# In-degrees of a graph layer: a stationary tile of ones and moving counts in place of products of two columns and transposes

## The chip, the cores and the metric

The kernel runs on one core of a Trainium2 chip. The metric is device time in microseconds (us), the median of several runs. A core has a tensor engine (PE, or TensorE; its weight loads are listed apart as PEld), a vector engine (DVE, or VectorE), a scalar engine (ACT, or ScalarE), GpSimd (POOL) and a sync engine (SP) that here issues the weight transfers. Each engine works through its own list of instructions in order and waits on semaphores for the others. Matrix products accumulate in PSUM, which has eight banks of 128 partitions x 512 float32 values.

## The reference, cut to what matters

One layer of a graph transformer on 625 nodes of 1024 features with 20000 edges: a layer norm, two graph convolutions beside a linear attention, then a mixture of experts. What the change touches is the in-degree of every node and its inverse:

```python
deg = segment_sum(ones_like(edge_dst), edge_dst, num_segments=N)     # N = 625
deg_inv = 1.0 / maximum(deg, 1.0)
h = relu(sage(x, src, dst, deg_inv, W_self0, W_neigh0, b0))
out = sage(h, src, dst, deg_inv, W_self1, W_neigh1, b1)
# sage: h @ W_self + (segment_sum(h[src], dst) * deg_inv[:, None]) @ W_neigh + b
```

Beside it stands the attention, whose queries and values are computed while the degrees are:

```python
q = softmax(q, axis=-1) * DH ** -0.5
k = softmax(k, axis=-2)
attn = q @ (k.T @ v) ; attn @ Wo + bo
```

## The kernel before, in words

The edges are counted into a matrix `ath` of 625 x 625 counts: `ath[source in tile s, s, destination]`, source nodes in partitions in five tiles (the last has 113 rows), destinations along the free dimension. The sum over an edge's sources is then a product with `ath`, and the in-degree of a destination is the sum of its column.

Every weight matrix passes through a stream: SP loads a block of 512 KB (`wraw`), ScalarE rounds it (`whi`), VectorE forms the rest (`wlo`), each in a ring of three buffers, and TensorE makes three products per pair of tiles (L206 to L208: high with high, low with high, high with low). `ts_half` computes one half (512 columns) of a product for all five node tiles in four units; a unit takes one block of weights and makes thirty products of 512 columns, six for each node tile. Five PSUM banks hold its sums, so three banks are left for everything else at that time. After each unit it can call a `step`.

The order of the stages around the change is: `unpack` (the counts become `ath`), the first half of the queries (`psq`), the second half with `queries_step` after each unit, the first half of the values (`psv`) and the second, with `values_step`; then the context product (`psc`, L727), the query product (`psa`, L744) and later the aggregation (`psag`, L804), which multiplies by `dinv` (L817), and the second convolution, which multiplies by `degs[:, 2]` (L874).

- `queries` (L665) is the softmax of a query half on VectorE and ScalarE: it reads each `psq` bank twice (L671, L672), which sets the bank free, and leaves five tiles `q`.
- `queries_back` (L658) transposes a `q` tile with four TensorE transposes (L662) into `psqt`; ScalarE copies it into `qt`. Each `step` takes two tiles.
- `degrees` (L546), called after unit 0 of the second query half, makes 25 products with a tile of `ath` stationary and two columns of ones moving, so that the degrees of a node tile come out in its own partitions, one column per tile. Two copies and `inverse_degrees` (four steps of `recip` behind a maximum, on 128 x 5) give `degs[:, 2]`.
- `look` (L559), after unit 1, sums the degrees and takes the largest packed count through two transposes and sets the flag `rare`, which is 1 or 2 if the packed counts did not hold the edges. All engines load the flag (L732) and branch on it (L733); the branch is not taken with these inputs.
- `inverse` (L627), after units 2 and 3 of the second half of the values, spreads 1/degree to all partitions with the destinations along the free dimension: five transposes of a broadcast column (L631) and two ScalarE copies give `dinv`.

A planner orders the instructions of each engine from the program's priorities, its dependences and its own estimates of times. PSUM tiles take any bank that is free at their turn.

Of the kernel before, what the change touches and what calls it, by code (L numbers as in the profile page):

```python
# [9 lines left out]
F32 = mybir.dt.float32  # L10
F32R = mybir.dt.float32r
# [5 lines left out]
ALU = mybir.AluOpType  # L17
AX = mybir.AxisListType

N = 625  # L20
T = 128
NT = -(-N // T)
NP = N + 1
# [25 lines left out]
PARTS = ((0, 314), (314, 312))  # L49
# [4 lines left out]
def rows(t):  # L54

    return slice(0, min(T, N - t * T))


def cols(t):

    return slice(t * T, min((t + 1) * T, N))
# [10 lines left out]
def gps_layer(ctx: ExitStack, tc: tile.TileContext, x, src, dst,  # L72
              ws0, wn0, b0, ws1, wn1, b1, wq, wk, wv, wo, bo,
              router_w, w1, w2, sgu, sdown, sgw, out):
    nc = tc.nc

    const = ctx.enter_context(tc.tile_pool(name="const", bufs=1))
    big = ctx.enter_context(tc.tile_pool(name="big", bufs=6))
    wts = ctx.enter_context(tc.tile_pool(name="wts", bufs=3))
    tmp = ctx.enter_context(tc.tile_pool(name="tmp", bufs=5))  # L80
# [12 lines left out]
    def bank(name="ps"):  # L93
        return psum.tile([128, 512], F32, name=name, tag="ps")
# [139 lines left out]
    ident = const.tile([128, 128], F32, name="ident")  # L234
# [56 lines left out]
    def recip(dsttile, a, scratch):  # L291
        nc.vector.reciprocal(dsttile, a)
        nc.vector.scalar_tensor_tensor(scratch, dsttile, -1.0, a, op0=ALU.mult, op1=ALU.mult)
        nc.vector.tensor_scalar(scratch, scratch, 2.0, None, op0=ALU.add)
        nc.vector.tensor_mul(dsttile, dsttile, scratch)
# [128 lines left out]
    with tc.high_priority():  # L424
# [38 lines left out]
                                 op0=ALU.mult, op1=ALU.add))  # L463
# [61 lines left out]
    ath = atp.tile([128, NT, XP], F32R, name="ath")  # L525
    degs = const.tile([128, 5, NT], F32, name="degs")
    nc.gpsimd.memset(degs, 0.0)
    two = const.tile([128, 2], F32R, name="two")
    nc.vector.memset(two.bitcast(F32), 1.0)

    def unpack():
        for s in range(NT - 1, 0, -1):
# [9 lines left out]
    def inverse_degrees():  # L542
        nc.vector.tensor_scalar(degs[:T, 1, :], degs[:T, 0, :], 1.0, None, op0=ALU.max)
        recip(degs[:T, 2, :], degs[:T, 1, :], degs[:T, 3, :])

    def degrees():  # L546
        ps = bank("psdg")
        for t in range(NT):
            for s in range(NT):
                nc.tensor.matmul(ps[rows(t), 2 * t:2 * t + 2], ath[rows(s), s, cols(t)], two[rows(s)],  # L550
                                 start=s == 0, stop=s == NT - 1)
        for a, b in ((0, NT - 1), (NT - 1, NT)):
            nc.vector.tensor_copy(degs[rows(a), 0, a:b],
                                  ps[rows(a), 2 * a:2 * b].rearrange("p (t k) -> p t k", k=2)[:, :, 0])
        inverse_degrees()

    rare = const.tile([1, 1], I32, name="rare")

    def look():  # L559


        nc.vector.reduce_sum(degs[:T, 4, 0:1], degs[:T, 0, :], axis=AX.X)
        ps = bank("psdm").rearrange("p (a b) -> p a b", b=128)
        for k in range(2):
            nc.tensor.transpose(ps[:1, k, :T], degs[:T, 4, k:k + 1], ident[:T, :T])
        few = const.tile([1, 2], F32, name="few")
        nc.vector.reduce_sum(few[:, 0:1], ps[:1, 0, :T], axis=AX.X)
        nc.vector.reduce_max(few[:, 1:2], ps[:1, 1, :T], axis=AX.X)
        nc.vector.tensor_scalar(few[:, 0:1], few[:, 0:1], float(E), None, op0=ALU.is_lt)
        nc.vector.scalar_tensor_tensor(rare, few[:, 1:2], 16.0, few[:, 0:1], op0=ALU.is_ge, op1=ALU.add)  # L570

    ard = dram.tile([NT * WIN, NP], F32, name="ard")
    atd = dram.tile([N, NP], F32R, name="atd")
# [1 line left out]
    def recount():  # L575

        acc = tmp.tile([128, NP], F32, name="acc", tag="tmp")
        sep = tmp.tile([128, 2, HW], F32, name="sep", tag="tmp")
        ct = tmp.tile([128, HW], F32, name="ct", tag="tmp")
        nc.vector.tensor_tensor(edst, edst, first_dst[:ET, None, :, None].to_broadcast([ET, 2, NG, CH // 2]), op=ALU.add)  # L580
        nc.vector.tensor_scalar(field[:ET], esrc, float(HW), None, op0=ALU.is_ge)
        nc.vector.scalar_tensor_tensor(esrc, field[:ET], -float(HW), esrc, op0=ALU.mult, op1=ALU.add)
        nc.vector.tensor_scalar(field[:ET], field[:ET], 4095.0, 1.0, op0=ALU.mult, op1=ALU.add)
        with tc.For_i(0, NT, 1) as r:
            nc.vector.memset(acc, 0.0)
            with tc.For_i(0, NG, 1) as g:
                ps = bank("pa")
                for i in range(CH):
                    h = tmp.tile([128, WIN + HW + 1], F16, name="hrare", tag="tmp")
                    nc.vector.tensor_scalar(h[:ET, :WIN], iota[:ET, :WIN], edst[:, i // 8, ds(g, 1), i % 8], None, op0=ALU.is_equal)  # L590
                    nc.vector.tensor_scalar(h[:ET, WIN:WIN + HW], iota[:ET, :HW], esrc[:, i // 8, ds(g, 1), i % 8],
                                            field[:ET, i // 8, ds(g, 1), i % 8], op0=ALU.is_equal, op1=ALU.mult)
                    nc.tensor.matmul(ps[:, :HW], h[:ET, :WIN], h[:ET, WIN:WIN + HW], start=i == 0, stop=i == CH - 1)
                nc.scalar.activation(ct, ps[:, :HW], AF.Identity, bias=mid, scale=2.0 ** -12)
                nc.vector.tensor_scalar(sep[:, 1, :], ct, MAGIC, None, op0=ALU.subtract)
                nc.vector.scalar_tensor_tensor(sep[:, 0, :], sep[:, 1, :], -4096.0, ps[:, :HW],
                                               op0=ALU.mult, op1=ALU.add)
                nc.vector.tensor_add(acc, acc, sep.rearrange("p a s -> p (a s)"))
            nc.gpsimd.dma_start(ard[ds(r * WIN, WIN), :], acc)
            nc.vector.tensor_scalar(edst, edst, float(WIN), None, op0=ALU.subtract)  # L600
        for j in range(NT):
            aj = tmp.tile([128, NP], F32, name="aj", tag="tmp")
            nc.gpsimd.dma_start(aj[rows(j)], ard[cols(j), :])
            for s in range(NT):
                ps = bank("psat")
                nc.tensor.transpose(ps[rows(s), rows(j)], aj[rows(j), cols(s)], ident[rows(j), rows(j)])
                al = tmp.tile([128, T], F32R, name="al", tag="tmp")
                split(ps[rows(s), rows(j)], ath[rows(s), s, cols(j)], al[rows(s), rows(j)])
                nc.gpsimd.dma_start(atd[cols(s), cols(j)], al[rows(s), rows(j)])
        for t in range(NT):  # L610
            pt = bank("psdt")
            for s in range(NT):
                al = tmp.tile([128, T], F32R, name="al", tag="tmp")
                nc.gpsimd.dma_start(al[rows(s), rows(t)], atd[cols(s), cols(t)])
                nc.tensor.matmul(pt[rows(t), :2], ath[rows(s), s, cols(t)], two[rows(s)], start=s == 0, stop=False)
                nc.tensor.matmul(pt[rows(t), :2], al[rows(s), rows(t)], two[rows(s)], start=False, stop=s == NT - 1)
            nc.vector.tensor_copy(degs[rows(t), 0, t:t + 1], pt[rows(t), 0:1])
        inverse_degrees()

# [7 lines left out]
    def inverse(t0, n):  # L627
        ps = bank("psd").rearrange("p (a b) -> p a b", b=128)
        for t in range(n):
            p = rows(t0 + t)  # L630
            nc.tensor.transpose(ps[:, t, p], degs[p, 2, t0 + t:t0 + t + 1].to_broadcast([p.stop, 128]), ident[p, p])  # L631
        c = slice(t0 * T, min((t0 + n) * T, N))
        nc.scalar.copy(dinv[:, c], ps.rearrange("p a b -> p (a b)")[:, :c.stop - c.start])
# [50 lines left out]
    def queries_step(u):  # L684
        for a in (next(back, None), next(back, None)):
            if a:
                queries_back(*a)
        if u == 0:
            degrees()
        elif u == 1:  # L690
            look()

    accs = [bank("psq") for _ in range(NT)]
    ts_half(xnh, xnl, accs, step=queries_step)
    back = iter(list(queries(1, accs)))
    mid_ctx = ExitStack()
    midp = mid_ctx.enter_context(tc.tile_pool(name="midp", bufs=1))
    dinv = midp.tile([128, NP], F32, name="dinv")


    def values_step(half, u):
        if half == 0:
            for a in (next(back, None), next(back, None)):
                if a:
                    queries_back(*a)
        elif u > 1:
            inverse(*((0, NT - 1), (NT - 1, 1))[u - 2])

    vnat = None
    for half in range(2):  # L710
# [12 lines left out]
    for o in range(KT):  # L723
        ps = bank("psc")
# [15 lines left out]
    for o in range(KT):  # L740
        for c0, n in PARTS:
            n = min(n, N - c0)
            ps = bank("psa")
# [9 lines left out]
    for half in range(2):  # L753
# [3 lines left out]
        for t in range(NT):  # L757
            xr = tmp.tile([128, 512], F32, name="xr", tag="tmp")
            p = rows(t)
# [18 lines left out]
    with tc.If(rare_v > 0, preferred_fallthrough_block=False):  # L778
        for s in range(NT):
            al = low_part(s)  # L780
            for o in range(KT):
                for c0, n in PARTS:
                    ps = bank("pslo")
                    c = slice(c0, min(c0 + n, N))
                    nc.tensor.matmul(ps[:, :n], g0h[rows(s), s, o * 128:(o + 1) * 128], al[rows(s), c0:c0 + n],
                                     start=True, stop=True)
# [42 lines left out]
    for half in range(2):  # L829
# [3 lines left out]
        for t in range(NT):  # L833
            p = rows(t)
# [3 lines left out]
    with tc.If(rare_v > 0, preferred_fallthrough_block=False):  # L838
        for s in range(NT):
            al = low_part(s)  # L840
            for t in range(NT):
                for half in range(2):
                    hs = slice(half * 512, (half + 1) * 512)
                    ps = bank("pslo")
                    p = rows(t)
# [396 lines left out]
    for i, r in enumerate(RANKS):  # L1242
        between = None
        if i < NE - 1:
            n = CAPS[RANKS[i + 1]]
# [73 lines left out]
```

## Time and profile before

| what | value |
|---|---|
| median of 3 runs | 1025.9 us (1025.32 to 1026.54) |
| the profiled execution's own time | 1026.03 us |
| its span, first to last instruction | 1024.5 us |
| mean granted clock of TensorE | 0.996 of full speed |
| TensorE busy | 1003.0 us, 98% |
| VectorE busy | 595.5 us, 58% |
| ScalarE busy | 395.4 us, 39% |
| GpSimd busy | 147.8 us, 14% |

The second query half begins at 177.85 us, the values at 211.9, their second half at 241.52, the context product at 269.29 and the query product at 279.22.

A line of the order of time gives the start, the duration (both in us), the engine, the line of the kernel, the operation and the tiles as out<-in; "128*128 128x2" is the stationary tile and then the output. Matrix products overlap, so that the distance from one start to the next is what one costs, not its duration. In a line of a group, the figures behind the bar are the busy time in us and the mean duration of one in ns, and then the engine's idle time ahead of them and what ended it. In a line of waits the figures are the total in us, how often, and the longest. In a line of stretches each engine has its busy time and number of instructions, in the order PE, PEld, DVE, ACT, POOL; then come the granted clock, the share of the transfer engines that was busy, and GB/s.

### The profile page before, as it was taken

What the parts mean: (1) busy time and instruction counts of PE and PEld (TensorE: products, weight loads), DVE (VectorE), ACT (ScalarE), POOL (GpSimd) and SP (SyncE); (2) the same over time, 40 slices, a digit from 0 to 9 for tenths busy, and PEclk for the clock granted to TensorE, in tenths of its full rate; (3) what the DMA queues carried; (4) which work ended last, traced back from release to release, by engine and by line L of the source; (5) the groups of instructions that cost most, each with busy time, mean ns of one, the idle gap of its engine ahead of it and who ended that gap; (6) DMA issues with size and microseconds to landing.
All of it is one profiled execution on the core that took longest, in us unless ns stands there. A gap on an engine that the chain in (4) does not pass through costs nothing. (4 is left out here: it accounts for less than half of the span.)

```text
span 1024.5 us, 14773 instructions
## 1 busy us (share of the span) xinstructions
PE 1003.0 (98%) x5557; PEld 863.4 (84%) x5557; DVE 595.5 (58%) x1207; ACT 395.4 (39%) x579; POOL 147.8 (14%) x206
## 2 busy tenths in 40 slices
PE   8999999999999999999999999999999989999998
PEld 6889998888878888988878999997978777887786
DVE  7999643572333325533337355458686788887681
ACT  5443242232221122222115332345646566766610
POOL 1000001110045100200001004213030033210120
PEclk9999999999999999999999999999999999999999
DMA  8022227664235321322230137566877898897861
GB/s 230 21 82 64 83 97 250 213 220 131 72 121 168 130 83 63 122 78 67 82 83 2 43 83 267 139 196 191 277 240 230 262 293 285 292 285 248 324 264 51
DMA packets 111464, 164.68 MB, mean 161 GB/s; under 512 B 5931, under 2 KB 63443, under 8 KB 111382
## 3 DMA queue, kind: packets, MB, share of 16 engines
q1 hardware_dynamic: 97734, 118.38, 36.8%
q0 software_dynamic: 13456, 45.08, 13.1%
q8 instruction: 47, 0.77, 0.3%
q14 instruction: 35, 0.29, 0.1%
q10 hardware_dynamic: 192, 0.16, 0.0%
HBM read 133.19 MB, written 30.42 MB: 160 GB/s over the span
## 5 line engine op out<-in xcount | busy, mean ns | idle before, releaser
L97 DVE TENSOR_TENSOR wlo<-wraw,whi 128x1024 fp32r<-128x1024 f32 x149 | 188.3, 1264 | 271.2 <-ACT whi L97 266.5
L97 ACT CAST whi<-wraw 128x1024 fp32r<-128x1024 f32 x149 | 156.6, 1051 | 310.5 <-PE psg L208 66.2
L1157 PE MATMUL pse<-xs,whi 128*128 128x448 f32 (+1 forms) x384 | 109.0, 357 | 0.0
L97 DVE TENSOR_TENSOR wlo<-wmore,whi 128x1024 fp32r<-128x1024 f32 x67 | 86.9, 1298 | 28.7 <-ACT whi L97 27.7
L1153 PE MATMUL pse<-xs,wlo 128*128 128x224 f32 (+1 forms) x384 | 89.7, 254 | 0.8 <-DVE wlo L97 0.8
L97 ACT CAST whi<-wmore 128x1024 fp32r<-128x1024 f32 x67 | 70.4, 1051 | 48.4 <-PE psz L208 17.9
L396 PE MATMUL psk<-xnh,whi 128*128 128x314 f32 (+3 forms) x256 | 82.5, 323 | 0.7 <-ACT xnh L97 0.7
L397 PE MATMUL psk<-xnl,whi 128*128 128x314 f32 (+3 forms) x256 | 79.7, 311 | 0.6 <-DVE xnl L97 0.6
L398 PE MATMUL psk<-xnh,wlo 128*128 128x314 f32 (+3 forms) x256 | 79.4, 310 | 0.0
L1153 PEld LDWEIGHTS pse<-xs,wlo 128*128 128x128 f32 x384 | 72.0, 190 | 1.9 <-DVE wlo L97 1.0
L1209 PE MATMUL psy<-wlo,he 128*128 128x512 f32 (+1 forms) x176 | 70.0, 398 | 3.3 <-DVE wlo L97 2.9
L1157 PEld LDWEIGHTS pse<-xs,whi 128*128 128x128 f32 x384 | 69.0, 189 | 2.4
L1208 PE MATMUL psy<-whi,he 128*128 128x512 f32 (+1 forms) x176 | 69.4, 395 | 0.0
L1210 PE MATMUL psy<-whi,he 128*128 128x512 f32 (+1 forms) x176 | 69.1, 392 | 0.0
L476 DVE TENSOR_SCALAR hot<-iota,srow,unit 125x128 f16<-125x128 f16 x160 | 51.7, 323 | 0.0
L97 POOL TENSOR_TENSOR xs<-raw,xs 128x512 fp32r<-128x512 f32 (+2 forms) x24 | 34.4, 1452 | 118.6 <-ACT xs L97 97.4
L396 PEld LDWEIGHTS psk<-xnh,whi 128*128 128x128 f32 x256 | 49.1, 192 | 1.2 <-ACT xnh L97 1.2
L397 PEld LDWEIGHTS psk<-xnl,whi 128*128 128x128 f32 x256 | 49.3, 193 | 0.8 <-DVE xnl L97 0.8
L398 PEld LDWEIGHTS psk<-xnh,wlo 128*128 128x128 f32 x256 | 49.1, 192 | 0.0
L1209 PEld LDWEIGHTS psy<-wlo,he 128*128 128x128 f32 (+1 forms) x176 | 31.8, 180 | 14.9 <-DVE wlo L97 6.7
L475 DVE TENSOR_SCALAR hot<-iota,edt 125x128 f16<-125x128 f16 x160 | 41.9, 262 | 0.2 <-issue 0.2
L1208 PEld LDWEIGHTS psy<-whi,he 128*128 128x128 f32 (+1 forms) x176 | 31.9, 181 | 10.1
(347 smaller groups left out, 2331.0 us busy)
## 6 DMA issues: line engine op xcount, KB each, us to landing
wraw<-in_L_ffn_w_dram SPq DMA_DIRECT2D x65, 512.0 KB, 5.0
wmore<-in_L_ffn_w_dram SPq DMA_DIRECT2D x63, 512.0 KB, 5.5
xsd<-zt POOLq DMA_DIRECT2D x9, 1024.0 KB
wraw<-in_L_gnn_W_self_dram SPq DMA_DIRECT2D x16, 512.0 KB, 3.9
wraw<-in_L_gnn_W_neigh_dram SPq DMA_DIRECT2D x16, 512.0 KB, 3.8
wraw<-_ffn_shared_gate_up_dram SPq DMA_DIRECT2D x16, 512.0 KB, 3.9
wraw<-in_L_mix_Wk_dram SPq DMA_DIRECT2D x8, 512.0 KB, 6.8
wraw<-in_L_mix_Wq_dram SPq DMA_DIRECT2D x8, 512.0 KB, 3.6
```

Source lines behind the costliest of these rows:

```text
L97: return (order(nc.scalar.copy(hi, srcap)), order((eng or nc.vector).tensor_sub(lo, srcap, hi.bitcast(F32))))
L396: nc.tensor.matmul(ps[:, :n], wh[:, kt, :], xnh[:, kt, c], start=kt == 0, stop=False)
L397: nc.tensor.matmul(ps[:, :n], wh[:, kt, :], xnl[:, kt, c], start=False, stop=False)
L398: nc.tensor.matmul(ps[:, :n], wl[:, kt, :], xnh[:, kt, c], start=False, stop=kt == KT - 1)
L475: nc.vector.tensor_scalar(h[:ET, :WIN], iota[:ET, :WIN], edst[e], None, op0=ALU.is_equal)
L476: return nc.vector.tensor_scalar(h[:ET, WIN:], iota[:ET, :WIN], srow[e], unit[e].bitcast(F32), op0=ALU.is_equal, op1=ALU.mult)
L1153: nc.tensor.matmul(ps[a][:, :n], wl[:, k, c], xs[:, kt, 0, :], start=False, stop=False)
L1157: nc.tensor.matmul(ps[a][:, :2 * n], wh[:, k, c], xs[:, kt], start=kt == 0, stop=kt == KT - 1)
L1208: nc.tensor.matmul(acc, h(kt, 0), wh[:, k, :], start=kt == 0, stop=False)
L1209: nc.tensor.matmul(acc, h(kt, 0), wl[:, k, :], start=False, stop=False)
L1210: nc.tensor.matmul(acc, h(kt, 1), wh[:, k, :], start=False, stop=kt == KT - 1)
```

## The change

`degrees` turns the product round: a tile of 128 x 128 ones is stationary and the counts move, 314 and then 312 columns of `ath` for each of the five source tiles. The sum of every column then stands in all 128 partitions at once, and the maximum and `recip` on it give `dinv` directly, 128 x 314 and 128 x 312. It is called after unit 2 of the second query half. `look` gets the column layout `degs[:, 2]` back from one row of `dinv` with five transposes, and does so after unit 3 of the values' first half together with the flag; `inverse` is now called only inside the branch that is not taken. The number of edges counted is summed from one partition of the product. `dinv` moves to the pool that lives throughout.

```diff
-    two = const.tile([128, 2], F32R, name="two")
-    nc.vector.memset(two.bitcast(F32), 1.0)
+    ones = const.tile([128, 128], F32R, name="ones")
+    nc.vector.memset(ones.bitcast(F32), 1.0)
+    dinv = const.tile([128, NP], F32, name="dinv")
...
+    few = const.tile([1, 4], F32, name="few")
+
     def degrees():
-        ps = bank("psdg")
-        for t in range(NT):
+
+        for i, (c0, n) in enumerate(PARTS):
+            ps = bank("psdg")
             for s in range(NT):
-                nc.tensor.matmul(ps[rows(t), 2 * t:2 * t + 2], ath[rows(s), s, cols(t)], two[rows(s)],
-                                 start=s == 0, stop=s == NT - 1)
-        for a, b in ((0, NT - 1), (NT - 1, NT)):
-            nc.vector.tensor_copy(degs[rows(a), 0, a:b],
-                                  ps[rows(a), 2 * a:2 * b].rearrange("p (t k) -> p t k", k=2)[:, :, 0])
-        inverse_degrees()
+                nc.tensor.matmul(ps[:, :n], ones[rows(s), :], ath[rows(s), s, c0:c0 + n], start=s == 0, stop=s == NT - 1)
+            nc.vector.reduce_sum(few[:, i:i + 1], ps[:1, :n], axis=AX.X)
+            deg = tmp.tile([128, 2, PARTS[0][1]], F32, name="deg", tag="tmp")
+            nc.vector.tensor_scalar(deg[:, 0, :n], ps[:, :n], 1.0, None, op0=ALU.max)
+            recip(dinv[:, c0:c0 + n], deg[:, 0, :n], deg[:, 1, :n])
 
     rare = const.tile([1, 1], I32, name="rare")
 
     def look():
 
-        nc.vector.reduce_sum(degs[:T, 4, 0:1], degs[:T, 0, :], axis=AX.X)
-        ps = bank("psdm").rearrange("p (a b) -> p a b", b=128)
-        for k in range(2):
-            nc.tensor.transpose(ps[:1, k, :T], degs[:T, 4, k:k + 1], ident[:T, :T])
-        few = const.tile([1, 2], F32, name="few")
-        nc.vector.reduce_sum(few[:, 0:1], ps[:1, 0, :T], axis=AX.X)
-        nc.vector.reduce_max(few[:, 1:2], ps[:1, 1, :T], axis=AX.X)
+        ps = bank("psdm")
+        for t in range(NT):
+            nc.tensor.transpose(ps[rows(t), t:t + 1], dinv[:1, cols(t)], ident[:1, :1])
+        for a, b in ((0, NT - 1), (NT - 1, NT)):
+            nc.vector.tensor_copy(degs[rows(a), 2, a:b], ps[rows(a), a:b])
+
+        nc.tensor.transpose(ps[:1, 128:128 + T], degs[:T, 4, 1:2], ident[:T, :T])
+        nc.vector.reduce_max(few[:, 2:3], ps[:1, 128:128 + T], axis=AX.X)
+        nc.vector.tensor_add(few[:, 0:1], few[:, 0:1], few[:, 1:2])
         nc.vector.tensor_scalar(few[:, 0:1], few[:, 0:1], float(E), None, op0=ALU.is_lt)
-        nc.vector.scalar_tensor_tensor(rare, few[:, 1:2], 16.0, few[:, 0:1], op0=ALU.is_ge, op1=ALU.add)
+        nc.vector.scalar_tensor_tensor(rare, few[:, 2:3], 16.0, few[:, 0:1], op0=ALU.is_ge, op1=ALU.add)
...
-        if u == 0:
+        if u == 2:
             degrees()
-        elif u == 1:
-            look()
...
-    dinv = midp.tile([128, NP], F32, name="dinv")
...
     def values_step(half, u):
         if half == 0:
             for a in (next(back, None), next(back, None)):
                 if a:
                     queries_back(*a)
-        elif u > 1:
-            inverse(*((0, NT - 1), (NT - 1, 1))[u - 2])
+            if u == 3:
+                look()
```

## The prediction

> **What bounds the kernel now.** I read the page's busy row first, then TensorE's waits around the change, then the stretches and the order of time where the removed instructions stand.
>
> ```profile
> PE 1003.0 (98%) x5557; PEld 863.4 (84%) x5557; DVE 595.5 (58%) x1207; ACT 395.4 (39%) x579; POOL 147.8 (14%) x206
> ```
>
> TensorE is busy for 1003.0 of 1024.5 us. Its waits from 150 to 280 us come to one line:
>
> ```profile
> PE psa L744 <- DVEq L733: 0.8, 1, 0.8
> ```
>
> So from the query product to the values, TensorE goes from product to product and sets the time: what is taken off it there is gained, what any other engine does costs nothing until TensorE waits for it. The stretches around the old degree products (busy time per engine, then granted clock, DMA share, GB/s):
>
> ```profile
> 185.64:188.40 2.76, 2.76 (x29) 2.76 (x27) 1.76 (x4) 2.02 (x4) 1.16 (x2) 1.00 0.08 2
> 190.00:191.00 1.00, 1.00 (x4) 0.81 (x3) 1.00 (x7) 0.00 (x0) 0.00 (x0) 0.50 1.05 418
> 191.00:192.00 1.00, 1.00 (x4) 0.81 (x3) 0.97 (x5) 0.00 (x0) 0.00 (x0) 0.50 1.03 412
> 193.00:194.00 1.00, 1.00 (x6) 0.79 (x6) 0.00 (x0) 0.00 (x0) 0.00 (x0) 1.00 0.87 303
> ```
>
> The same in order of time (start, duration):
>
> ```profile
> 185.67 2.87 PE L550 MATMUL psdg<-two,ath 128*128 128x2 f32 x25
> 188.40 0.47 PE L206 MATMUL psq<-whi,xnh 128*128 128x512 f32 x1
> 188.71 0.39 PE L207 MATMUL psq<-wlo,xnh 128*128 128x512 f32 x1
> ...
> 189.17 0.56 PE L206 MATMUL psq<-whi,xnh 128*128 128x512 f32 x1
> ...
> 190.39 0.63 PE L206 MATMUL psq<-whi,xnh 128*128 128x512 f32 x1
> 190.82 0.63 PE L207 MATMUL psq<-wlo,xnh 128*128 128x512 f32 x1
> ...
> 192.82 0.40 PE L206 MATMUL psq<-whi,xnh 128*128 128x512 f32 x1
> ```
>
> Two things are to be seen. The 25 products of two columns take 2.73 us from start to start (188.40 - 185.67), 109 ns each, which is a weight load and hardly any streaming. And less than a microsecond later the clock is halved: wide products that start every 0.227 us elsewhere start every 0.43 us, until 192.8.
>
> **TensorE, part by part.** Removed:
> - The 25 products: 2.73 us.
> - The half clock after them: nine products start between 189.17 and 192.82, 3.65 us, where nine at 0.227 take 2.04. Lost: 1.61 us.
> - Five transposes that spread 1/degree (L631) and two in look() (L565). The first four:
>
> ```profile
> 261.92 0.60 PE L631 MATMUL psd<-ident,degs 128*128 128x128 f32 x4
> 262.27 0.48 PE L206 MATMUL psv<-whi,xnh 128*128 128x512 f32 x1
> 262.59 0.39 PE L207 MATMUL psv<-wlo,xnh 128*128 128x512 f32 x1
> ```
>
> Four take 0.35; the first wide product behind any such group takes 0.32 to the next, 0.09 more than 0.227, which I call a switch. The fifth stands 0.10 (269.19 to 269.29), the two of look() 0.14 (197.79 to 197.93). With the switch: 0.68 us.
>
> Added:
> - Ten products with the ones stationary and 314 or 312 columns of `ath` moving. The nearest rows are the aggregation's, same moving tile:
>
> ```profile
> 402.69 0.46 PE L804 MATMUL psag<-ath,g0h 128*128 128x314 f32 x2
> 402.99 0.46 PE L804 MATMUL psag<-ath,g0l 128*128 128x314 f32 x2
> ```
>
> Two every 0.294 us, so 0.147 each and 1.47 us for ten.
> - Five transposes of one row into one column load 128 columns of weights and stream one. No row has this form; it lies between 0.0875 (L631) and 0.109 (the two-column products): 0.5 us. The sixth is like one of L565: 0.07. They stand at two places in the second half of the values: two switches, 0.18. Bounds for all six: 0.55 to 0.95.
> - In the built order the groups of eight query transposes in the values' first half are cut into four and four, twice: two switches, 0.18.
>
> Sum: 2.73 + 1.61 + 0.68 - 1.47 - 0.75 - 0.18 = 2.62 us. Without the clock term it is 1.01.
>
> **The clock term, row against rule.** The row shows a 0.50 clock for about 3.4 us right behind the narrow products, and no other dip between 36 and 1020 us; eight query transposes alone (218.90) bring none, nor do 9 us of products of 128 columns in the context stage (L727). I conclude that the run of narrow products causes it. The Trainium skill, "TensorE: Matmul & The Clock Gate", Part 1, speaks against counting on it: the clock goes to half after a window of some 3.4 us in which TensorE was idle, and the window runs freely, so that it falls differently in each run. Here TensorE was not idle (2.76 of 2.76 us busy by the profile), and a gap has to fall well in a window: by the rule taken literally the products are not the cause, the dip might stay, and the gain is 1.01. By the row it is 2.62. I take the row; that the timed runs have the dip as well is likely but not shown (they spread over 1.2 us, less than 1.61).
>
> **VectorE.** It gains work in the tight place. Removed are two small copies, the five steps on 128x5 and two sums, some 0.07 to 0.3 us each, at 188 to 192 and 199 us; VectorE idles 6.1 us after them, so nothing is gained. Added, per half: a sum in one partition, a maximum, and reciprocal, two corrections and a product, all 314 wide. In the built order all twelve stand between the low-part split and the query back-work, which frees the PSUM banks that the values need:
>
> ```profile
> 206.20 1.22 DVE L97 TENSOR_TENSOR wlo<-wraw,whi 128x1024 fp32r<-128x1024 f32 x1 [6.10 <-ACT whi L97]
> 207.34 0.68 DVE L671 TENSOR_REDUCE qm<-psq 128x8 f32<-128x512 f32 x1
> ...
> 219.68 1.22 DVE L97 TENSOR_TENSOR wlo<-wraw,whi 128x1024 fp32r<-128x1024 f32 x1
> ```
>
> Count from 204.88, where the transposes after unit 2 of the second query half start. VectorE is free at 2.46. The ten steps other than reciprocals: 0.48 for 314 elements from PSUM (L817), 0.81 for 625 in L795 and L376, 0.48 for 626 in L536, so 0.25 to 0.41 from start to start each, 3.7 in all. The reciprocals are known only narrow:
>
> ```profile
> L292 DVE RECIPROCAL qm<-qm 128x8 f32<-128x8 f32 x8 | 1.5, 197 | 0.0
> L259 DVE RECIPROCAL lnt<-lnt 128x1 f32<-128x1 f32 x5 | 0.8, 162 | 1.1 <-ACT lnt L257 1.0
> ```
>
> 35 ns for seven more elements, 5.0 ns each: 314 take 0.16 + 1.57 = 1.73 us. Against this the skill's "VectorE: DVE Perf Modes", section "Walkthrough: the 8-slice pipeline in each mode", has the reciprocal divide iteratively with a repeat count of 8; at the 0.96 GHz of "Trainium Kernel Development and Optimization" (NeuronCore Architecture) I estimate 8.3 ns an element, 2.8 us. Lower end: one that streams like the others, 0.48.
>
> TensorE's deadlines on the same count: transposes 0.31, ten products 1.47, a switch, 30 products of unit 3 (6.8): values begin at 8.7. Eighteen products use three banks that are free (the two degree banks are read by about 6.5): 12.8. Then a bank is needed whose query tile VectorE has read twice. By the row VectorE gets there at 2.46 + 3.7 + 3.4 + 0.61 + 0.68 = 10.8; the next bank, needed at 14.4, is free at 13.3; the low part of the values' unit 2, needed at 23.9, is ready at 22.4 (11.7 us of queries before it, read off the lines above). Slack 2.0, 1.1 and 1.5: no wait. By the page everything is 2.1 later: about 12.9, 15.4 and 24.5, so TensorE waits some 0.6 to 1.0 us and the gain is 1.6 to 2.0. If that cover were gone entirely, all 7.1 us would show.
>
> **Others.** ScalarE loses two copies (0.58, 0.25) at 263 and 270; it waits for TensorE around them: nothing. The flag `rare` comes at about 244 instead of 200. On SP its load now stands behind the second Wo block; behind it is the third, issued near 251: hidden by 6 us. On POOL nothing stands behind it but the branch, which holds it to 279.67 anyway (46.17 us idle). The sixth transpose waits for a copy queued behind the last values copy on VectorE (241.72 + 0.69, then 0.2); TensorE gets to it 1.7 us into the half begun at 241.52, 243.2: 0.6 of slack. No DMA is added.
>
> **Result.** The profiled execution took 1026.03 us (span 1024.5), 0.13 above the median of 1025.9. 1026.03 - 2.62 = 1023.4; from the median, 1023.3. I give 1023.3, own range 1022.4 to 1023.9.
>
> **Rivals.**
> - The clock gain isn't there: the timed runs of before lack the dip, or one stays. For: the free-running window. Against: the records, and timed runs close to the profiled one. 1025.9 - 1.0 = 1024.9.
> - VectorE is late by a little: reciprocals near the page's figure, TensorE waits up to 1.0 us or, with a further 0.5 of slack lost, 1.5. 1024.0 to 1024.8; I write 1024.4.
> - Slower, by the same queue: each ns per element of the two reciprocals delays the banks by 0.63 us. The slack of 1.1 is gone at 6.7 ns, the gain at about 11, and 0.2% (2.05 us, about what a measurement of this kernel can tell from no change) is lost at 14. At 15 ns: 6.3 - 1.1 - 2.6 = 2.6 us, 1028.5. For: no wide reciprocal in the trace, and it stands ahead of everything the values wait for. Against: 5.0 ns in the rows.
>
> **How the numbers follow.** Forecast 0.52; no clock gain 0.18; a little late 0.14; slower 0.10; a gain above 3.4 us, if the transposes cost less and the dip cost more than I counted, 0.06. Faster by over 0.2% means below 1023.85: most of the first and the last, 0.52. Slower 0.10, the rest 0.38. The range runs over the first three and the bounds of the transposes: 1022.0 to 1026.0; left out are the slower case and the extremes.
>
> **What would show it.** A PEclk of 1.00 from 180 to 200 us; ten products every 0.147 us; reciprocals of 1.7 us; no TensorE wait on VectorE between 200 and 230. It is wrong if wide products start every 0.43 us somewhere new, if the values' first unit shows a gap before its fourth tile, or if the reciprocals take over 2.6 us.

## The result: 1029.95 us, 0.4% slower, and where the time went

The changed kernel takes 1029.95 us (median, 1028.35 to 1030.5) against 1025.9 us (1025.09 to 1027.65) of the kernel before: ratio 1.0037, 95% interval 1.0027 to 1.0048. Forecast were 1023.3 us and a range of 1022.0 to 1026.0. The profiled execution took 1029.5 us, with a span of 1027.9.

What the change does in its own place came out as forecast. TensorE's row of the page, the order of time around the new products, the group of reciprocals, and the stretches that were at half clock before:

```profile
PE 1003.4 (98%) x5541; PEld 862.6 (84%) x5541; DVE 604.8 (59%) x1213; ACT 395.3 (38%) x577; POOL 148.4 (14%) x206
```

```profile
199.59 1.71 PE L554 MATMUL psdg<-ath,ones 128*128 128x314 f32 x10
201.14 0.40 PE L206 MATMUL psq<-whi,xnh 128*128 128x512 f32 x1
201.37 0.39 PE L207 MATMUL psq<-wlo,xnh 128*128 128x512 f32 x1
```

```profile
L292 DVE RECIPROCAL dinv<-deg 128x314 f32<-128x314 f32 (+1 forms) x2 | 4.2, 2090 | 0.0
```

```profile
190.00:191.00 1.00, 1.00 (x6) 0.79 (x5) 0.00 (x0) 0.00 (x0) 0.00 (x0) 1.00 1.10 434
191.00:192.00 1.00, 1.00 (x8) 0.81 (x7) 0.00 (x0) 0.18 (x1) 0.00 (x0) 1.00 0.93 326
```

Ten products take 1.55 us (201.14 - 199.59), the granted clock (the figure after POOL) is 1.00 where it was 0.50, and from the first query product (149.8 us) to the query product `psa` (275.4) 125.6 us pass; before it was 128.4 (150.8 to 279.2). So 2.8 us were won where 2.62 were forecast. By the time of the gate and up products the changed kernel is 3.8 us ahead (555.1 against 558.9; 1.0 of it lies ahead of the queries, where the profiles of all runs differ by 1.5 us, 149.8 to 151.4, so it is not to be put down to the change).

All of it, and more, is lost far behind, in code that the change does not touch. TensorE's waits name the places:

```profile
PE psz L207 <- issue: 2.5, 1, 2.5
...
PE psup L218 <- issue: 1.5, 2, 1.1
```

"Issue" is time in which the engine waited for nothing that the profile shows. Before, there is one such wait in the up product, 0.7 us, and none in `psz`, the last product of the kernel. In order of time, first the up product, then the place behind the last branch (it jumps over an overflow pass, which these inputs do not need):

```profile
626.85 0.34 PE L220 MATMUL psup<-xfh,wlo 128*128 128x384 f32 x1
627.56 0.38 PE L218 MATMUL psup<-xfh,whi 128*128 128x242 f32 x1 [0.38 <-issue]
...
628.27 0.27 PE L220 MATMUL psup<-xfh,wlo 128*128 128x242 f32 x1 [0.22 <-issue]
629.67 0.34 PE L218 MATMUL psup<-xfh,whi 128*128 128x384 f32 x1 [1.13 <-issue]
```

```profile
964.55 0.47 PE L206 MATMUL psz<-whi,sth 128*128 128x512 f32 x1 [1.45 <-DVEq L1259]
967.54 0.39 PE L207 MATMUL psz<-wlo,sth 128*128 128x512 f32 x1 [2.53 <-issue]
967.77 0.40 PE L208 MATMUL psz<-whi,stl 128*128 128x512 f32 x1
```

The same place in the kernel before, where the second product follows in 0.31 us:

```profile
965.42 0.47 PE L206 MATMUL psz<-whi,sth 128*128 128x512 f32 x1 [1.45 <-DVEq L1257]
965.73 0.39 PE L207 MATMUL psz<-wlo,sth 128*128 128x512 f32 x1
965.96 0.40 PE L208 MATMUL psz<-whi,stl 128*128 128x512 f32 x1
```

And behind each of the two gaps in the changed kernel the clock is halved for 3.41 us (the stretches 631 to 632 and 969 to 970):

```profile
631.00:632.00 1.00, 1.00 (x6) 1.00 (x5) 0.72 (x1) 0.52 (x2) 0.00 (x0) 0.50 1.01 412
969.00:970.00 1.00, 1.00 (x4) 0.81 (x3) 0.00 (x0) 0.00 (x0) 0.83 (x1) 0.50 1.05 401
```

The account of the two profiles: 3.8 us ahead at 555, 0.2 ahead at 678 (3.5 lost in the gate and up products), 0.9 ahead at 964.5, then 4.3 lost within fifteen products: 3.4 us behind, which is the difference of the spans. (The 0.7 between 678 and 964.5 says little: from the last up product to the first `psz` product the profiles of all runs take between 285.9 and 288.0 us, with no order by kernel.)

### The profile page after: what moved, and what is told of

It is laid out like the page before. It is cut to its first block, busy times and chain, and to the rows that moved or that the text cites. A ratio compares the mean times of both kernels' runs of the same rounds, so it can differ in the third digit from the quotient of the medians.

```text
span 1027.9 us, 14746 instructions
## 1 busy us (share of the span) xinstructions
PE 1003.4 (98%) x5541; PEld 862.6 (84%) x5541; DVE 604.8 (59%) x1213; ACT 395.3 (38%) x577; POOL 148.4 (14%) x206
## 5 line engine op out<-in xcount | busy, mean ns | idle before, releaser
L476 DVE TENSOR_SCALAR hot<-iota,srow,unit 125x128 f16<-125x128 f16 x160 | 49.2, 308 | 0.0
L218 PE MATMUL psup<-xfh,whi 128*128 128x384 f32 (+1 forms) x128 | 40.1, 314 | 1.5 <-issue 1.5
```

What stands on the lines that cost most here:

```text
L218: nc.tensor.matmul(ps[:, :n], wh[:, kt, :], xh[:, kt, c], start=kt == 0, stop=False)
L476: return nc.vector.tensor_scalar(h[:ET, WIN:], iota[:ET, :WIN], srow[e], unit[e].bitcast(F32), op0=ALU.is_equal, op1=ALU.mult)
```

## Experiments: what stops TensorE in code that was not changed

The instructions behind the change are the same in both kernels, and in the same order. What differs is where they stand: TensorE's list has 16 products fewer (x5557 and x5541, each with its own weight load) and two semaphore instructions fewer, so everything behind stands 34 instructions earlier. VectorE's list is 7 longer. The Trainium skill, "Runtime: NRT & Kernel Launch", section "Instruction fetch mechanics", says that an engine reads its instructions in blocks of 16 KiB, 256 instructions, one ahead, that crossing an edge is mostly hidden, and that a branch to a target outside of the blocks it holds waits for a fetch. The trace has these fetches as a queue of their own; one falls into the gap (the transfer view of 965.0 to 967.5 us; packets, MB, share; other engines' code comes on q14, 8192 bytes at a time, which would be 128 instructions by the page's size):

```profile
q8 instruction: 1, 0.02, 2.8%
```

Theory L: the change moved the edge of a block right behind the last branch's target, and TensorE waits there for its code; the half clock follows from that gap. The one fetch does not show it yet: the kernel before has one at the same place (965.60 to 966.72 us) and no wait. Rival T: the gaps come from the work being some 3.8 us earlier, or from what the change executes. To move code without executing anything, products were put into (or left out of) `recount`, the branch that these inputs never take.

### Moving TensorE's code back: e1, e3

```diff
 def recount():
     ...
     inverse_degrees()
+    pad = bank("pad")
+    for i in range(17):          # e3: 64
+        nc.tensor.matmul(pad[:, :2], ones, ones[:, :2], start=i == 0, stop=i == 17 - 1)
```

> The changed kernel with 17 more TensorE products (34 instructions) written into the recount that stands behind the branch that is never taken. They are not executed; they only move the code of everything behind the branch to where it stood before the change, because the change made TensorE's list 34 instructions shorter. Theory L (place of the code: the edge of an instruction block falls right behind the last branch's target, and TensorE waits there for its instructions): the gap of 2.5 us ahead of the second product behind the last branch is gone (0.3 us or less) and the half clock behind it too: 1022.5 to 1023.5 us, up to 1025.5 if the stall during the scatter in the gate and up stage stays. Rival T (the stalls come from the work being about 3.8 us earlier, or from what the change executes, not from where the code stands): 1029.5 to 1030.5 us, with both stalls.

> The changed kernel with 64 products (128 instructions, half a block) in the branch that is never taken, so that the edge of a block stands about half a block from the last branch's target. Theory L: no gap behind the last branch: 1022 to 1025.5 us, depending on what the stall during the scatter does. Rival T: 1029.5 to 1030.5 us.

Measured: 1025.37 us and 1025.69 us (before on the same chip 1025.93). In both the second `psz` product follows without a gap and there is no half clock. For this gap T is out: both kernels execute what the changed kernel executes. But neither is at the 1023 us that the local gain gives: in both the up product stalls 2.5 us, before 0.85.

Because the level of that stall turned out to vary (below), the changed kernel and e1 were run side by side:

> The changed kernel once more, beside the three that follow on the same chip, since the stall during the scatter came out between 0 and 2.6 us in kernels that ran on two different chips. As first measured: about 4 us over the kernel before, with a gap of 2.5 us behind the last branch, and some 2.6 us of stall during the scatter.

> e1_pad17 once more (TensorE's code moved back, VectorE's not): 0.5 us under the kernel before if its level is its own; 2 to 3 us under it if its stall of 2.6 us belonged to the other chip.

Measured on one chip: 1025.96 and 1021.94 us, before 1025.35. Neither profile has a stall in the up product, and from the first `psz` product to the last one r_after takes 3.74 us longer than r_e1 (58.03 against 54.29): that is the gap with its half clock, and the medians' 4.0 is that within the differences between executions. With its code in the old place the change wins 3.4 us (ratio 0.9971, interval 0.9962 to 0.9981), 0.6 more than the 2.8 of its own place; the kernel before was timed but not profiled on this chip, so where the rest comes from stays open.

### Moving the code of the kernel before: e2, e10

e2 puts 111 products (222 instructions, 256 with the 34) into the branch of the kernel before; e10 leaves 17 out of it.

```diff
 # e2
+        pad = bank("pad")
+        for i in range(111):
+            nc.tensor.matmul(pad[:, :2], xnh[:, 0, :128], two, start=i == 0, stop=i == 111 - 1)
 # e10
-                nc.tensor.matmul(pt[rows(t), :2], ath[rows(s), s, cols(t)], two[rows(s)], start=s == 0, stop=False)
+                if s == 0 or 4 * t + s - 1 >= 17:
+                    nc.tensor.matmul(pt[rows(t), :2], ath[rows(s), s, cols(t)], two[rows(s)], start=s == 0, stop=False)
```

> The kernel before with 111 more TensorE products (222 instructions; with the 34 of the change one block of 256) written into the branch that is never taken. None is executed: the kernel does what it did, but the code behind the branch stands, within its blocks of 256 instructions, where it stands in the changed kernel. Theory L: a gap of about 2.5 us behind the last branch and a half clock of 1.6 us after it: about 1030 us, 1032 if a stall during the scatter appears too. Rival T: 1025.9 us, with neither.

> The kernel before with 17 of the TensorE products of the recount left out, that is 34 instructions of the branch that is never taken (with these inputs nothing else changes): TensorE's code behind the branch stands exactly where it stands in the changed kernel, and no branch becomes longer. Theory L: a gap of 2 to 2.8 us behind the last branch, a half clock after it, no gap at the first branch: 4.0 us over the kernel before, 1029.4 us. Rival T: as the kernel before, 1025.4 us.

e10 took 1030.77 us, before 1025.87 (ratio 1.0041, interval 1.0029 to 1.0053), with a program that executes exactly what the kernel before executes. Its waits and its order of time show the gap that the change has:

```profile
PE psz L207 <- issue: 2.9, 1, 2.9
```

```profile
965.47 0.47 PE L206 MATMUL psz<-whi,sth 128*128 128x512 f32 x1 [1.61 <-ACTq L1258]
968.80 0.58 PE L207 MATMUL psz<-wlo,sth 128*128 128x512 f32 x1 [2.85 <-issue]
969.18 0.63 PE L208 MATMUL psz<-whi,stl 128*128 128x512 f32 x1
969.61 0.63 PE L206 MATMUL psz<-whi,sth 128*128 128x512 f32 x1
```

The whole `psz` product lasts 4.97 us longer than in the kernel before (59.26 against 54.29, first start to last): 3.02 until the second product, 1.95 from the half clock, which lasted 6.83 us in this execution. L holds in both directions.

The fetches say how. In the five profiles with the gap (those of after, r_after, e9, e10 and e2) no fetch on q8 begins in the 29 us ahead of the first `psz` product; the next one begins between 0.01 us before it and 1.04 us after it, and the second product follows 1.2 to 1.4 us after that fetch has ended, whether that was early or late (966.29 and 967.54 us in the first profile of the changed kernel, 961.10 and 962.46 in r_after). In the fifteen profiles without the gap a fetch had ended 2.6 to 14 us before the first `psz` product.

e2 took 1036.1 us, 6 more than expected, and its waits say why:

```profile
PE psa L747 <- issue: 3.9, 1, 3.9
...
PE psz L207 <- issue: 2.3, 1, 2.3
```

The longer branch cost 3.9 us and another half clock ahead of the query product, at the first branch. The 64 products of e3 in the same branch did not (no such wait), 111 did, and so did the 120 of e4. It is not the place of the edge: within its blocks e2 stands there as the changed kernel does and e4 as e1 does, and neither of those waits. So a longer jump has its own price, and e2 cannot price the gap behind the last branch; e10 does.

### The half clock behind the narrow products: e4, e11

```diff
+    def narrow():
+        ps = bank("psold")
+        for t in range(NT):
+            for s in range(NT):
+                nc.tensor.matmul(ps[rows(t), 2 * t:2 * t + 2], ath[rows(s), s, cols(t)], ones[rows(s), :2],
+                                 start=s == 0, stop=s == NT - 1)
...
+        if u == 0:
+            narrow()
         if u == 2:
             degrees()
```

e4 has 120 products in the dead branch, e11 leaves 8 out instead; both put the code behind the branch, within its blocks, where e1 has it.

> The changed kernel that also executes the 25 old products of two columns at their old place (their sums are not used), and has 120 products in the branch that is never taken so that the code behind it stands, within its blocks, as in the run with 17. Against that run: the products cost 2.7 us, and if a run of such products is what halves the clock behind it (the step of the prediction that went by the row), another 1.6 us with a half clock near 188 to 193 us: 4.3 us more. If the dip in the kernel before was not theirs: 2.7 us more and no dip. Theory T expects the same differences, from a higher level (about 1030).

> e1_pad17 a third time: 2.5 to 3.5 us under the kernel before if the scatter's stall is absent, 0.5 us under it if it is 2.5 us.

> The changed kernel with the 25 old products of two columns executed as well (sums not used), and 8 products left out of the branch that is never taken, so that TensorE's code behind it stands as in e1 and in the kernel before. Against r2_e1: 2.7 us for the products and 1.6 us for the half clock behind them, 4.3 us; 2.7 us if the half clock is not theirs.

e11 took 1028.83 us and e1, on the same chip, 1024.56: 4.27 us, where 4.3 were expected. Its order of time and stretches:

```profile
185.65 2.87 PE L564 MATMUL psold<-ones,ath 128*128 128x2 f32 x25
188.38 0.47 PE L206 MATMUL psq<-whi,xnh 128*128 128x512 f32 x1
```

```profile
189.50:190.50 1.00, 1.00 (x4) 0.81 (x3) 0.90 (x4) 0.00 (x0) 0.00 (x0) 0.50 1.02 399
193.00:194.00 1.00, 1.00 (x6) 0.80 (x5) 0.00 (x0) 0.00 (x0) 0.00 (x0) 1.00 0.88 342
```

2.73 us for the products and a clock of 0.50 behind them. In all eight profiles that have the 25 products this half clock begins between 187.5 and 189.3 us; the twelve without them have none from 180 to 200. e4 (1034.79 us) shows the same locally but also the 3.6 us wait at the first branch, so its total says nothing on this point.

### The slack of VectorE: e7

```diff
+            nc.vector.reciprocal(dinv[:, c0:c0 + n], deg[:, 0, :n])
             recip(dinv[:, c0:c0 + n], deg[:, 0, :n], deg[:, 1, :n])
```

> e1_pad17 with each of the two wide reciprocals executed twice, one behind the other: 4.2 us more on VectorE ahead of everything that the values wait for (the planner also places some query transposes otherwise, and the VectorE list is 2 longer). By the prediction's sum the bank's slack of 1.1 us is 0.4 with the measured 2.09 us: TensorE waits some 3.8 us in the values' first units: 1029 us. If the slack was larger than counted, less: at 4.6 us of slack nothing, 1025.4 us.

```profile
L292 DVE RECIPROCAL dinv<-deg 128x314 f32<-128x314 f32 (+1 forms) x2 | 4.2, 2082 | 0.0
L558 DVE RECIPROCAL dinv<-deg 128x314 f32<-128x314 f32 (+1 forms) x2 | 4.1, 2062 | 0.0
```

It took 1023.98 us, before 1025.7 (0.9981, 0.9974 to 0.9988), and not the 1029 expected. VectorE was 4.1 us busier ahead of the values' banks, and TensorE's list of waits has none in the values (one product is 0.26 us late, at 225.38 us). But this is not a slack of 4 us. The planner took the longer work into account and put TensorE's products in another order. The second read that frees the second bank, and the second product of the fifth node tile (the one with 113 rows), in the changed kernel and then in e7:

```profile
212.25 0.67 DVE L677 TENSOR_TENSOR q<-psq,qm 128x512 f32<-128x512 f32 x1
...
213.84 0.39 PE L207 MATMUL psv<-wlo,xnh 128*113 128x512 f32 x1
```

```profile
217.70 0.67 DVE L681 TENSOR_TENSOR q<-psq,qm 128x512 f32<-128x512 f32 x1
...
219.45 0.39 PE L207 MATMUL psv<-wlo,xnh 128*113 128x512 f32 x1
```

That product is the 27th of the values in the changed kernel and the 45th in e7, so the banks are needed later there. The slack of the kernel as built is read off its own profile: the first bank has been read twice at 210.53 us and is written from 212.02, the second at 212.92 and from 213.61. That is 1.5 and 0.7 us, where 2.0 and 1.1 were counted.

### The stall during the scatter: e5, e6, e8, e9

The second loss stands where GpSimd's ten scatter transfers (619 us before, 615 after) run beside the gate and up weights. Before, VectorE has a wait for its own instructions just there; after, it has none. From e5, which has VectorE's code where it was:

```profile
618.18 1.23 DVE L97 TENSOR_TENSOR wlo<-wraw,whi 128x1024 fp32r<-128x1024 f32 x1 [0.31 <-issue]
```

Theory V: the 7 extra VectorE instructions moved that edge, and this decides the stall. Tried with dead VectorE work in the same branch:

```diff
+        for i in range(118):     # e5, e9: 121 instructions with their semaphores; e6: 6 (7); e8: 60
+            nc.vector.memset(ct[:, :8], 0.0)
```

e5 and e8 are e1 with it, e6 is the kernel before with it, e9 the changed kernel with it alone.

> The changed kernel with 17 dead TensorE products (as in e1_pad17) and dead VectorE work too, 121 instructions, in the branch that is never taken: with the 7 that the change adds to VectorE's list they make 128, so that VectorE's code behind the branch, too, stands within its blocks as before the change. Theory V (the scatter stage loses 2.6 us instead of 0.9 because the edge of a block of VectorE's code has moved: before, VectorE waits 0.31 us for its instructions just ahead of a low-part split during the scatter, which moves the next weight load against the scatter): the 0.31 us wait is back, the stall in the up product is about 0.9 us, and the time is 1023.5 to 1024.0 us. Rival A (the stall comes from what the change executes or from where its tiles lie in memory): as e1_pad17, 1025.4 us with 2.6 us of stall.

> The kernel before with 7 dead VectorE instructions in the branch that is never taken: VectorE's code behind it stands as in the changed kernel; nothing else differs, and none is executed. Theory V: no 0.31 us wait of VectorE during the scatter, 2.6 us of stall in the up product in place of 0.9, and 1027.6 us. Rival A: 1025.9 us with 0.9 us of stall.

> e1_pad17 with some 60 dead VectorE instructions in the same branch, half a block: the edge of VectorE's block is then far from the scatter on either side. Theory V in its narrow form (only a VectorE wait at just that split spares the stall): 2.6 us of stall, 1025.4 us. If any place but the changed kernel's is good: 0.9 us or less, 1023.5 us. Rival A: 1025.4 us.

> e5_pad_both once more (both codes moved back): 3 us under the kernel before. If VectorE's code place is what counts for the stall during the scatter, 1.5 us or more below r_e1 on this same chip; if the chip did it, equal to r_e1 within 0.5 us.

> The changed kernel with VectorE's code alone moved back (121 dead instructions), TensorE's left as the change made it. If the two places count each for itself: the gap behind the last branch with its half clock stays (4 us), the stall during the scatter is as in r_e5; so r_e5 plus 4 us, about 1 us over the kernel before. If VectorE's place does nothing: as r_after.

> The kernel before, profiled beside the next three on the same chip. If the stall during the scatter belongs to the chip, it is the same here (within 0.5 us) as in the run r2_e1. If it belongs to the kernel, it is 0.84 us as in its first profile, whatever r2_e1 shows.

> e5_pad_both again, beside the next. If VectorE's place decides: less stall during the scatter than in r3_e6, by 1.2 to 1.6 us (0.9 against 2.4 on a chip such as that of e1, 0 against 1.25 on one such as that of its first run); if the executed kernel decides: more stall than r3_e6 by as much; on a chip without the stall: none in either.

> e6_before_dve7 again (the kernel before with VectorE's place of the changed kernel). If the place decides: 1.2 to 1.6 us of stall more than r3_e5, and 1.4 us over the kernel before; if the executed kernel decides: 0.9 us of stall and as the kernel before.

Times (the kernel before on the same chip in brackets): e5 1022.36, e6 1025.65, e8 1022.94 (1025.7); r_e5 1021.97, e9 1026.51 (1025.35); r3_e5 1023.05, r3_e6 1026.33 (1025.35). The stall itself, as the time that the 46 products around it last longer than in r_e5, which has none:

| chip | VectorE's code as before | as in the changed kernel, or elsewhere |
|---|---|---|
| A | the kernel before: r2_before 0.84, e2 0.91, e10 1.03 | the changed kernel: e1 2.46 and 2.39 (r2_e1), e3 2.46, e4 2.43, e11 2.34 |
| B | the changed kernel: e5 0.01 and 0.53 (r3_e5) | the kernel before: e6 1.26 and 1.11 (r3_e6); the changed kernel: e7 1.48, e8 1.16 |
| C | r_e5, e9: 0.00 | r_after, r_e1: 0.00 |

A, B and C are the chips of the experiments; that of the first two profiles is not on record.

Two things follow. For one kernel on one chip the stall repeats within 0.5 us, and it differs between chips: on C nothing stalls. And in the profiles of B it goes with VectorE's place: the changed kernel stalls 0.6 to 1.5 us less in the old place (e5) than in others (e7, e8), and the old kernel in the new place (e6) stalls as those do. On A place and kernel were not separated. The first step of V is in every profile: behind VectorE's 0.31 us wait the next weight load is issued 3.0 us after the first scatter transfer (eight profiles, VectorE's old place), otherwise 2.7 us (twelve).

In the timed runs V is not shown: r3_e5 and r3_e6 differ by 3.3 us, 0.5 more than the 2.8 of the change itself, but e6 was equal to before in its first run and could not be told from it (1.0008, interval 0.9999 to 1.0017) in its second, where 1.4 us or more were expected. The kernel before was not profiled on B. On C, where nothing stalls, r_e5 and r_e1 are equal; e8, whose place is neither of the two, stalls like the new one. e9 came out 4.5 us over r_e5 on C, near the 4 us of the gap and its half clock; with no stall there, it says nothing on VectorE's place.

What TensorE waits for in that stall is not settled, but ScalarE's activation of the gate sum narrows it. In the changed kernel's first profile, in the same kernel on chip C, and in e5 on chip B, where TensorE does not stall (0.01 us):

```profile
629.82 0.49 ACT L933 ACTIVATE sgt<-psga 128x384 f32<-128x384 f32 x1 [8.77 <-remote]
```

```profile
625.94 0.49 ACT L933 ACTIVATE sgt<-psga 128x384 f32<-128x384 f32 x1 [4.44 <-PE psga L220]
```

```profile
630.69 0.49 ACT L938 ACTIVATE sgt<-psga 128x384 f32<-128x384 f32 x1 [8.56 <-remote]
```

The last product of the bank that it reads ends at 625.46, 625.91 and 626.53 us. On C ScalarE starts 0.03 us later, in the other two 4.4 and 4.2 us later. The trace's record of TensorE's semaphore shows why: in sixteen of the twenty profiles it has no update for 10.7 to 10.9 us at this place, though products that make one have ended, and the next comes 14.3 to 14.5 us after the first scatter transfer is issued, whichever kernel it is and wherever its code stands. In the other four, r_after, r_e1, r_e5 and e9 on chip C, the updates come on time.

So TensorE's signals are late while the scatter runs, in e5 too; VectorE's place does not change that, but only whether TensorE itself stalls meanwhile. In the changed kernel's first profile TensorE goes on at 629.67, and the late update comes at 629.80. That the scatter holds the signals up, and how a shift of 0.3 us in a weight load changes TensorE's stall, was not tested: no run here took the scatter away.

## Why the prediction was wrong, step by step

- **Removed products, half clock.** Right: 2.73 us and 1.61 us were forecast, and e11 pays 4.27 for both. Between row and rule, the row was the right choice: 8 of 8 profiles with the narrow products have the half clock, 0 of 12 without. The rule of a window of some 3.4 us in which TensorE is idle (the Trainium skill, "TensorE: Matmul & The Clock Gate", Part 1) fits the gaps only loosely: all five profiles with the gap behind the last branch have a half clock behind 2.0 to 2.9 us of waiting, which is shorter, and of six stalls of 2.3 us or more during the scatter only one was followed by one.
- **Ten wide products.** 1.55 us against 1.47. **Transposes.** The five of one row take 0.44 us (L566, 237.59 to 238.03), within the bounds taken. The whole local sum, 2.62, came out at 2.8.
- **VectorE.** The reciprocals were mis-sized: 2.09 us measured, 1.73 taken from the row, 2.8 estimated from the Trainium skill's "VectorE: DVE Perf Modes", "Walkthrough: the 8-slice pipeline in each mode". From eight to 314 elements that is 6.2 ns an element ((2.09 - 0.197) / 306), between the 5.0 of the row and the 8.3 of the page. The slack was counted rightly to within 0.5 us: 1.5 and 0.7 where 2.0 and 1.1 were forecast, while the two reciprocals took 0.7 more. TensorE has no wait in the values, so the rival that ends slower through this queue did not come.
- **The step that failed** is the result line, "1026.03 - 2.62". It carried a local gain to the end of the kernel on the sentence that what is taken off TensorE between the queries and the values "is gained". Every term was a duration; none was for the length of the instruction lists, which the same diff changes: 34 instructions off TensorE's, 7 onto VectorE's. In its place the runs show 4.0 us for the block edge behind the last branch (r_after against r_e1 on C; 4.9 in e10 on A), and up to 3 us more of stall in the scatter stage, depending on the chip (3.90 us with its half clock in the first profile, 0.85 before). The cause of the first is shown; that VectorE's place adds to the second is seen in profiles alone, and why anything stalls there is open.
- **The direction of the sum.** -2.8 + 4.0 leaves 1.2 us slower, and the stall brings the first comparison to 4.05. On chip C, without any stall in the changed kernel's profile, it is 0.6 us over the kernel before (1.0010, interval 1.0000 to 1.0019).
- **What would show it wrong** named "wide products start every 0.43 us somewhere new"; that is what stands at 631 and 969 us. Its cause was not among the rivals.
- **A version that is faster than both** is e5, the change with both lists put back in place by dead code: 0.9973 (0.9964 to 0.9983), 0.9970 (0.9961 to 0.9979) and 0.9972 (0.9963 to 0.9981) on chips B and C, 2.3 to 3.4 us under the kernel before; on A it was not run. e1 alone, with TensorE's list put back, gives 0.9996 (A), 0.9971 (C) and 0.9992 (A).

## What to carry to other kernels

In a kernel with branches, an edit that changes the number of instructions of the engine that sets the time moves every block edge behind it; a gain of a few microseconds is worth comparing only after looking behind each branch for a gap of kind "issue", and some dead instructions in a branch that is not taken can put the edge elsewhere, if they are few (17 products here; 111 made the jump itself dear). A small loss that appears in code that was not touched is best tested by moving the code of the kernel before to the same place. And a time on one chip can hide a stall that another chip does not have: compare against the kernel before on the same chip, and profile both there.

## What was not expected of the hardware

- The edge of a block of instructions right behind a taken branch cost TensorE 2.0 to 2.9 us of waiting (five profiles: after 2.5, r_after 2.0, e9 2.8, e10 2.9, e2 2.3), and 3.7 to 5.5 us with the half clock behind it. The Trainium skill, "Runtime: NRT & Kernel Launch", section "Instruction fetch mechanics", calls crossing an edge mostly hidden; right behind a branch these runs show otherwise.
- A jump over 222 or more further instructions cost 3.6 and 3.9 us at its target (e4, e2); over 128 further ones it cost nothing.
- Twenty-five products of two columns, with TensorE busy throughout by its record, are followed by 3.41 us at half clock, in eight profiles of eight.
- The same program stalls 2.4 us at one place on one chip and not at all on another (e1: 2.46 and 2.39 on A, 0.00 on C). While ten scatter transfers run, TensorE's signal to ScalarE comes 4.1 to 4.4 us behind the end of its product in sixteen profiles and on time in the four of chip C.
